# A scratch write between indirect gathers in a two-layer graph kernel

## The chip, the cores and the metric

The kernel runs on one core of a Trainium2 chip. The metric is the device time in microseconds of one execution; lower is better. Besides the times there is a profile of one execution: what each engine ran and when, what ended each wait, and what the DMA queues moved. The engines are named as the profile names them: PE is TensorE (PEld its weight loads), DVE is VectorE, ACT is ScalarE, POOL is GpSimd, SP is SyncE. L191 is line 191 of the kernel before.

## What is computed

A graph of N = 2708 nodes with 128 features each goes through two layers. Each is followed by a residual sum and a normalization over the features. `adj` is a row-normalized adjacency matrix with few entries other than zero in most rows.

Layer 0 is hyperbolic: a product with a 128 x 128 matrix with tanh, artanh and norms around it, then `adj` times the result, then row-wise functions. Layer 1 sends messages along the edges:

```python
s = node_feats @ msg_w[:, :D].T
d = node_feats @ msg_w[:, D:].T
messages = gelu(s[:, None, :] + d[None, :, :] + msg_b)
aggregated = einsum('ijd,ij->id', messages, adj)
new_feats = concatenate([node_feats, aggregated], -1) @ upd_w.T + upd_b
h = gelu(new_feats) + node_feats          # then a layernorm
```

The messages are needed only where `adj[i, j]` is not zero. So the kernel finds the edges, gathers the rows of `d` that belong to them, and works on tiles of 128 edges.

## The kernel before

The nodes lie in NB = 22 blocks of 128. The work has three stages in one program.

*Layer 0, with the search for edges.* For each block b, SP loads a slab `aT` of the transposed adjacency (1.4 MB, L317). TensorE multiplies it with `y` in 22 steps (L324). Beside this ScalarE takes the sign of the slab (L319), and TensorE and VectorE turn the signs into sorted lists of edge positions: `keys` (L350, L358) and `extract`. In `extract` the number of edges per node is summed over the partitions by two small matmuls (L397, L398), ScalarE copies the sums out (L399), VectorE builds 0/1 matrices `R` that assign edge slots to nodes (L409 to L414), and matmuls with `R` (L438) bring each slot its position, from which VectorE works out (L441 to L448) a column index `J` and a flat address `F`. There are 25 lists in all, with 1 to 8 tiles each, 99 tiles together. `F` has three buffers, so a list's addresses can be written only when the gathers of the list three before have taken theirs.

*The end of layer 0* (`layer0_end`) runs in two chunks, blocks 0 to 15 and 16 to 21. It ends with the rows of `d` being written to a table in DRAM by SP (L535), and `s` in `mx` (L534).

*Messages.* For each tile of 128 edges, `dd` receives 128 rows of the table. TensorE spreads `s` over the edge slots (L686), VectorE adds the two (L691), ScalarE applies Gelu (L692), and a matmul with `rv` (built at L688 from the weights `V`) adds the messages up per node (L694). Up to four tiles go together. `dd` comes from a ring of seven buffers, and for the first eight blocks from a slab as well. After each block come the update matmuls (L605 to L608), Gelu (L609), the normalizations and the store (L640). For the first eight blocks the tiles whose columns lie in the first chunk are done ahead, as soon as the table holds these rows.

*The gathers.* GpSimd issues all 198 of them through one helper, `gather`. Ninety-nine fetch one weight of `adj` for each of 128 edges into a column of `V` (L452, 4 bytes for each partition); ninety-nine fetch 128 rows of 512 bytes from the table into `dd` or the slab (L685). They are indirect DMAs: GpSimd makes the descriptors, and the DMA queue moves the data. A gather of `V` waits for its `F`; a gather of `dd` waits for a free buffer; from the ninth on each also waits for the gather eight before it to have landed, since eight semaphores go round.

The order of instructions on each engine is set when the program is built: a scheduler places them by priority and by an estimate of when they become ready, and within an engine they run in that order. `tc.issue_after(ins)` makes the instructions traced inside it stand behind `ins` in the queue of the same engine. It puts them in order; it does not make them wait for the data of a DMA.

Two constants of the setup matter for the change: `ones` (128 x 128 of 1.0, L121) and `nhalf` (one column of -0.5, L124). The last group of the kernel already uses GpSimd for a power, `ve ** -0.5`, at L599, twice, on two columns.

Of the kernel before, what the change touches and what calls it, by code (L numbers as in the profile page):

```python
# [10 lines left out]
F32 = mybir.dt.float32  # L11
# [4 lines left out]
OP = mybir.AluOpType  # L16
AX = mybir.AxisListType

P = 128
# [56 lines left out]
def hyperbolic_then_message_kernel(  # L76
# [10 lines left out]
    nc = tc.nc  # L87
# [11 lines left out]
    const = ctx.enter_context(tc.tile_pool(name="const", bufs=1))  # L99
# [21 lines left out]
    ones = const.tile([P, P], F32, name="ones")  # L121
    nc.gpsimd.memset(ones, 1.0)

    nhalf = const.tile([P, 1], F32, name="nhalf")  # L124
# [62 lines left out]

    of_block = {b: [l for l, v in enumerate(LISTS) if v[0] == b] for b in range(NB)}

    def gather(o, src, at):  # L190
        nc.gpsimd.indirect_dma_start(  # L191
            out=o, out_offset=None, in_=src, in_offset=bass.IndirectOffsetOnAxis(ap=at, axis=0)
        )

    mx = big.tile([P, NB, D], F32, name="mx")
    y = big.tile([P, NB, D + 2], F32, name="y")
# [169 lines left out]
    def extract(l):  # L366
# [84 lines left out]
        for t in range(t0, t0 + n):  # L451
            gather(V[:, t : t + 1], adj.rearrange("i (j o) -> (i j) o", o=1), F[:, t - t0 : t - t0 + 1])  # L452
# [87 lines left out]
    last = {}  # L540
# [135 lines left out]
    def messages(b, ag, tiles, first, final, bins, room=ring):  # L676

        for q, k0 in enumerate(range(0, len(tiles), 4)):
            ts = tiles[k0 : k0 + 4]
            w = len(ts)  # L680
            dd = room(w)
            X = bank(bins[q % len(bins)]).rearrange("p (t d) -> p t d", d=D)[:, :w, :]
            rv = edge.tile([P, 4, P], F32, name="rv", bufs=3)
            for k, t in enumerate(ts):
                gather(dd[:, k, :], table[: SPLIT * P] if t in soon else table, J[:, t : t + 1])  # L685
                nc.tensor.matmul(X[:, k, :], lhsT=R[:, t, :], rhs=s_nm[:, b, :], start=True, stop=True)  # L686

                nc.vector.tensor_scalar(  # L688
                    rv[:, k, :], iotaN, rid[:, t : t + 1], V[:, t : t + 1], op0=OP.is_equal, op1=OP.mult
                )  # L690
            nc.vector.tensor_tensor(dd, X, dd, op=OP.add)  # L691
            nc.scalar.activation(dd, dd, AF.Gelu)  # L692
            for k in range(w):
                nc.tensor.matmul(  # L694
                    ag[:, :P],
                    lhsT=dd[:, k, :],
                    rhs=rv[:, k, :],
                    start=(first and k0 == 0 and k == 0),
                    stop=(final and k0 + k == len(tiles) - 1),
                )  # L700
            step()
# [193 lines left out]
```

## Time and profile before

| | |
|---|---|
| device time, median of 3 runs | 491.01 us (484.5 to 493.97) |
| device time of the profiled execution | 477.53 us |
| span of the profiled execution | 475.8 us |
| granted TensorE clock, mean | 0.83 |
| gathers into V, into dd, into the slab | 99, 81, 18 |
| start of the first and of the last gather | 47.13 and 435.62 us |

The span runs from the first to the last instruction. It splits into a start (to 47 us, where the inputs land and the first list is made), layer 0 with the search (to 253 us, where the first gather from the table starts), the messages (to 437 us, the last gather) and a tail of 39 us. The busy time of each engine in these stretches, in microseconds:

| stretch | PE | DVE | ACT | POOL | granted clock |
|---|---|---|---|---|---|
| 0 to 47 | 26.5 | 33.7 | 24.8 | 11.5 | 0.82 |
| 47 to 132 | 59.2 | 42.3 | 34.2 | 43.4 | 0.86 |
| 132 to 212 | 74.8 | 54.0 | 51.2 | 34.4 | 1.00 |
| 212 to 253 | 37.7 | 34.0 | 28.1 | 8.8 | 0.96 |
| 253 to 437 | 98.4 | 88.0 | 46.5 | 102.9 | 0.73 |
| 437 to 475.8 | 17.0 | 29.7 | 14.2 | 1.4 | 0.76 |

How to read the lines that follow. A group of instructions has its line, engine, operation, what it writes and reads, and a count; after the bar its busy time and the mean of one in ns; after the second bar the idle time of the engine just before these instructions, and what ended most of it. A wait names the instruction that waited, what released it, and the total, the number and the longest. "Remote", or "another core or an unknown queue", means that a semaphore ended the wait and the profile found no instruction that had raised it just then. "Issue" is a wait for which no semaphore was found. On POOL the recorded spans are rough.

### The profile page before, as it was taken

How to read it: one execution, taken by the hardware profiler on the slowest of the kernel's cores; microseconds unless marked ns; L12 is line 12 of the kernel's file. 1: busy time of each engine (PE TensorE's matmuls, PEld its weight loads, DVE VectorE, ACT ScalarE, POOL GpSimd, SP SyncE). 2: the span in 40 equal slices, each digit the busy share in tenths (PEclk: the TensorE clock that was granted, in tenths of full speed). 3: DMA queues.
4: the chain of work that ended last, by engine and by line, in shares of the span. 5: the costliest groups of instructions: out<-in, count | busy, mean ns of one | idle time of the engine just before them, and what ended most of it. 6: DMA issues, size and time to landing. Idle time of an engine off the chain costs nothing.

```text
span 475.8 us, 7804 instructions
## 1 busy us (share of the span) xinstructions
PE 313.6 (66%) x2427; PEld 283.2 (60%) x2427; DVE 281.7 (59%) x1517; ACT 199.0 (42%) x538; POOL 202.4 (43%) x297
## 2 busy tenths in 40 slices
PE   4259778871799999979797402052839755878830
PEld 4259667771789989879686301031839655767720
DVE  1998655552476666689874234714827534566992
ACT  2836344441357565579375111115513311122540
POOL 5300555654454534322225574771351657564001
PEclk9759988977899999999899565575777959789975
DMA  8406322331245544533342011121020112111111
GB/s 331 206 2 214 107 74 95 124 122 44 80 167 201 181 186 160 207 123 123 139 140 72 22 51 31 41 72 28 21 47 12 39 39 53 38 45 34 45 40 39
DMA packets 16236, 45.13 MB, mean 95 GB/s; under 512 B 5626, under 2 KB 11150, under 8 KB 13374
## 3 DMA queue, kind: packets, MB, share of 16 engines
q1 hardware_dynamic: 9710, 37.43, 21.8%
q0 software_dynamic: 6336, 6.55, 5.8%
q10 hardware_dynamic: 144, 0.60, 0.4%
q8 instruction: 20, 0.33, 0.3%
q14 instruction: 26, 0.21, 0.1%
HBM read 41.74 MB, written 2.83 MB: 94 GB/s over the span
## 4 chain that ended last, share of the span: by engine, by line
DVE 29%; PE 25%; another core or an unknown queue 17%; issue 14%; ACT 8%; DMA 4%; POOL 1%; DVEq 0%; POOLq 0%; ACTq 0%
PE mp L324 5%; PE X L686 4%; PE sel L438 3%; PE mp L694 3%; ACT sgn L319 3%; PE kx L350 2%; DVE top L358 2%; DMA V<-in_adj_dram,F 2%; DVE rv L688 2%; PE ag L694 1%; DMA xT<-in_x_t_dram 1%; POOL V L191 1%; PE sel L608 1%; DVE st L592 1%
## 5 line engine op out<-in xcount | busy, mean ns | idle before, releaser
L191 POOL DMA_INDIRECT V<-in_adj_dram,F x99 | 95.1, 961 | 148.9 <-DVE mid L402 34.7
L324 PE MATMUL mp<-y,aT 128*128 128x130 f32 x968 | 127.7, 286 | 1.1 <-DVE y L308 0.9
L324 PEld LDWEIGHTS mp<-y,aT 128*128 128x128 f32 x968 | 118.6, 198 | 1.9 <-DVE y L308 1.1
L191 POOL DMA_INDIRECT dd<-table_dram,J x81 | 76.9, 950 | 76.1 <-issue 20.3
L319 ACT ACTIVATE sgn<-aT 128x2816 bf16<-128x2816 f32 x22 | 56.0, 2548 | 23.1 <-issue 19.0
L438 PE MATMUL sel<-z,R 128*128 128x49 f32 (+4 forms) x198 | 30.8, 295 | 35.8 <-DVE R L412 12.8
L438 PEld LDWEIGHTS sel<-z,R 128*128 128x128 f32 x198 | 27.7, 210 | 38.3 <-DVE R L412 13.0
L686 PE MATMUL X<-mx,R 128*128 128x128 f32 x198 | 35.7, 325 | 17.2 <-DVE mx L534 7.3
L350 PEld LDWEIGHTS <-sgn 128*128 128x128 bf16 x484 | 32.5, 108 | 19.2 <-issue 10.5
L350 PE MATMUL kx<-kd,sgn 128*128 128x128 bf16 x484 | 38.2, 238 | 7.8 <-ACT sgn L319 7.5
L686 PEld LDWEIGHTS X<-mx,R 128*128 128x128 f32 x198 | 31.5, 235 | 19.0 <-DVE mx L534 7.5
L358 DVE MAX8 top<-kx 128x8 f32<-128x128 f32 (+3 forms) x152 | 28.6, 235 | 22.5 <-remote 14.1
L688 DVE TENSOR_SCALAR rv<-iotaN,rid,V 128x128 f32<-128x128 f32 x99 | 30.3, 341 | 14.0 <-remote 6.5
L441 DVE TENSOR_TENSOR work<-sel,place 128x144 f32<-128x144 f32 (+11 forms) x29 | 11.7, 403 | 42.7 <-remote 30.6
L409 ACT ACTIVATE work<-iota,mid 128x512 f32<-128x512 f32 (+3 forms) x53 | 26.8, 553 | 11.2 <-issue 5.7
L444 ACT COPY rid<-sel 128x3 f32<-128x3 f32 (+5 forms) x29 | 4.7, 162 | 55.2 <-DVE work L441 52.3
L691 DVE TENSOR_TENSOR dd<-X,dd 128x384 f32<-128x384 f32 (+3 forms) x29 | 15.1, 524 | 19.5 <-remote 14.8
L694 PE MATMUL mp<-rv,dd 128*128 128x128 f32 x116 | 21.0, 325 | 6.2 <-issue 4.4
L397 PE MATMUL sel<-db,tri 128*128 128x2 bf16 x25 | 4.2, 168 | 27.8 <-ACT db L396 11.8
L694 PEld LDWEIGHTS mp<-rv,dd 128*128 128x128 f32 x116 | 17.9, 229 | 7.6 <-issue 5.1
L692 ACT ACTIVATE dd<-dd 128x384 f32<-128x384 f32 (+3 forms) x29 | 14.0, 499 | 18.8 <-DVE dd L691 15.0
L191 POOL DMA_INDIRECT aT<-table_dram,J x18 | 17.5, 971 | 5.5 <-issue 5.5
(204 smaller groups left out, 580.0 us busy)
## 6 DMA issues: line engine op xcount, KB each, us to landing
aT<-in_adj_t_dram SPq DMA_DIRECT2D x22, 1408.0 KB, 7.2
V<-in_adj_dram,F POOLq DMA_INDIRECT x99
xT<-in_x_t_dram SPq DMA_DIRECT2D x2, 704.0 KB
x_sb<-in_x_nm_dram SPq DMA_DIRECT2D x2, 704.0 KB
out_dram<-nom SPq DMA_DIRECT2D x21, 64.0 KB, 1.6
dd<-table_dram,J POOLq DMA_INDIRECT x81
table_dram<-dt SPq DMA_DIRECT2D x5, 256.0 KB
pk<-in_pack_dram ACTq DMA_DIRECT2D x1, 587.5 KB
```

Of the source, the lines that this page charges most:

```text
L191: nc.gpsimd.indirect_dma_start(out=o, out_offset=None, in_=src, in_offset=bass.IndirectOffsetOnAxis(ap=at, axis=0))
L319: nc.scalar.activation(sgn, aT, AF.Sign, accum_out=signs[:, b : b + 1])
L324: nc.tensor.matmul(op[:, : D + 2], lhsT=aT[:, j, :], rhs=y[:, j, :], start=(j == 0), stop=(j == NB - 1))
L350: nc.tensor.matmul(kp[:, i * P : (i + 1) * P], lhsT=sgn[:, j, :], rhs=kd[:, q, :], start=False, stop=(i == len(groups) - 1 and j == j1 - 1),)
L358: nc.vector.max(top[:, c : c + 8], seg[:, s, :])
L409: nc.scalar.activation(r0, iota[:, k0 * P : k1 * P], AF.Abs, scale=2.0, bias=mid[:, k : k + 1])
L438: nc.tensor.matmul(sp[:, k, :], lhsT=R[:, t0 + k0 + k, :], rhs=z, start=True, stop=True)
L686: nc.tensor.matmul(X[:, k, :], lhsT=R[:, t, :], rhs=s_nm[:, b, :], start=True, stop=True)
L688: nc.vector.tensor_scalar(rv[:, k, :], iotaN, rid[:, t : t + 1], V[:, t : t + 1], op0=OP.is_equal, op1=OP.mult)
L691: nc.vector.tensor_tensor(dd, X, dd, op=OP.add)
L692: nc.scalar.activation(dd, dd, AF.Gelu)
L694: nc.tensor.matmul(ag[:, :P], lhsT=dd[:, k, :], rhs=rv[:, k, :], start=(first and k0 == 0 and k == 0), stop=(final and k0 + k == len(tiles ...
```

## The change

After each gather GpSimd computes one scratch column, `1.0 ** -0.5` for each of the 128 partitions, which nothing reads. The instruction stands directly behind its gather in GpSimd's queue, so that two gathers no longer follow one another at once. All writes go to the same column `gap`, so each also waits for the one before it. The numbers that the kernel computes stay as they are.

```diff
+    gap = const.tile([P, 1], F32, name="gap")
+
     def gather(o, src, at):
-        nc.gpsimd.indirect_dma_start(
+        last = nc.gpsimd.indirect_dma_start(
             out=o, out_offset=None, in_=src, in_offset=bass.IndirectOffsetOnAxis(ap=at, axis=0)
         )
+        with tc.issue_after(last.ins):
+            nc.gpsimd.tensor_tensor(gap, ones[:, :1], nhalf, op=OP.pow)
```

## The prediction

> **What bounds the kernel now.** I read the page first, then the chain of waits, the waits by engine, and the timeline of the places that they name.
>
> ```profile
> PE 313.6 (66%) x2427; PEld 283.2 (60%) x2427; DVE 281.7 (59%) x1517; ACT 199.0 (42%) x538; POOL 202.4 (43%) x297
> DVE 29%; PE 25%; another core or an unknown queue 17%; issue 14%; ACT 8%; DMA 4%; POOL 1%; DVEq 0%; POOLq 0%; ACTq 0%
> L191 POOL DMA_INDIRECT V<-in_adj_dram,F x99 | 95.1, 961 | 148.9 <-DVE mid L402 34.7
> L191 POOL DMA_INDIRECT dd<-table_dram,J x81 | 76.9, 950 | 76.1 <-issue 20.3
> ```
>
> No engine is full, and GpSimd carries 1% of the chain. But 17% of the span, 81 us, hangs on a releaser that the profile cannot name, in a program of one core. The waits by engine say who sits there ("remote" is the same thing):
>
> ```profile
> DVE work L441 <- remote: 30.6, 6, 10.7
> DVE dd L691 <- remote: 14.8, 6, 3.8
> DVE top L358 <- remote: 14.1, 6, 3.9
> ACT dt L532 <- remote: 12.5, 2, 8.1
> ACT nom L609 <- remote: 11.8, 3, 5.7
> ACT oe L399 <- remote: 10.1, 1, 10.1
> ```
>
> The columns are the total, the times and the longest wait. None of these instructions uses what a gather brings in, L691 apart. ACT L399 copies the result of a matmul at L398. The timeline of that place (start, duration, engine, line):
>
> ```profile
> 105.53 0.16 PE L398 MATMUL sel<-db,ones_b 128*128 128x2 bf16 x1
> 106.45 0.95 POOL L191 DMA_INDIRECT V<-in_adj_dram,F  x1 [0.30 <-issue]
> 107.70 0.94 POOL L191 DMA_INDIRECT V<-in_adj_dram,F  x1 [0.30 <-issue]
> 108.94 0.94 POOL L191 DMA_INDIRECT V<-in_adj_dram,F  x1 [0.30 <-issue]
> 110.19 0.94 POOL L191 DMA_INDIRECT V<-in_adj_dram,F  x1 [0.30 <-issue]
> 111.44 0.94 POOL L191 DMA_INDIRECT V<-in_adj_dram,F  x1 [0.30 <-issue]
> 112.69 0.94 POOL L191 DMA_INDIRECT V<-in_adj_dram,F  x1 [0.30 <-issue]
> 116.02 0.16 ACT L399 COPY oe<-sel 128x2 f32<-128x2 f32 x1 [10.13 <-remote]
> ```
>
> The matmul ends at 105.69; its reader starts at 116.02. In between only gathers run, one each 1.25 us. The same picture stands at 52.4 (L438 is done, L441 starts at 55.76, the last gather of that burst at 53.74) and between 279 and 291, where even VectorE's waits for its own results take 1.8 us each. So my reading is: while gathers follow one another, the signals of the other engines arrive late, often only about 2 us after the last gather has started. The profile shows the coincidence, not the mechanism.
>
> The second thing to see is how much slack the gathers have. The timeline of line 691 shows the first quad used at 332.42, its first gather issued at 253.21; the last column is gathered at 435.62 and used at 451.72, 16 us later.
>
> **What the Trainium skill says.** "Perfetto Trace Analysis", section on the SWDGE DMA instruction: the recorded end of such a DMA is the end of descriptor generation, not the landing. The trace agrees: a row lasts 0.94 us, while the chain of waits has a piece of 2.18 us (at 294.36) from issue to landing. The same page, section on GPSIMD engine instructions, says to trust start-to-start spacing rather than spans; I do so below. "SBUF — State Buffer", section on the two sides: a GpSimd instruction that reads SBUF and a VectorE instruction with two SBUF inputs exclude each other for the whole instruction. The new instruction reads two columns, so it can hold up such VectorE work for its own length; before, nothing in the trace tests this. I found no page that says that gathers delay signals.
>
> **The change part by part.** In the order of the built program the other four engines keep their instructions in the same order with the same waits. GpSimd's list goes from gather after gather to gather, power, gather, power: 198 TENSOR_TENSOR on one column are added. Each but the first also waits for GpSimd's own counter, which the power before it raised. Nothing reads the column.
>
> *The price of one pair.* Gather to gather is 1.245 us now (0.944 busy and 0.30 before it). The nearest row to the new instruction is the power at L599 on two columns, 698 and 730 ns, 714 in the mean. A one-column GpSimd instruction (L148) takes 190 ns. If the rest of L599 is per column, one column costs 0.19 + (0.714 - 0.19)/2 = 0.45; if it is fixed, 0.71. I take the middle, 0.58. Two dependent GpSimd instructions at 7.1 and 7.4 us stand 0.08 apart. The pair is 0.94 + 0.08 + 0.58 + 0.30 = 1.90 us. The ends: 1.6, if the 0.30 before a gather passes beside the power, and 2.15, with the dear power and 0.2 in place of 0.08.
>
> *Work added.* 198 x 0.65 = 129 us on GpSimd, about 273 us idle now. Queued behind each power is the next gather, and behind that those who use V and dd. By stage:
>
> - 47 to 253 us: 90 gathers need 90 x 1.90 = 171 of 206 us, so they fit. The waits ended by "remote" here are 19.9 on L441, 10.1 on L399 and 10.2 on L358. The last fall after 132, where TensorE is busy 75 of 80 us and then 38 of 41, so they give back little. Between 47 and 132 TensorE is busy 59.2 of 85: up to 26 us can come back. But 45 gathers at 1.90 need 85 us there, and F has three buffers, so list l waits for the gathers of list l-3. I take 15 of the 26, and 3 us from the end of the first chunk (231 to 246). The first table gather then starts at 253 - 18 = 235.
> - 253 to 437 us: 108 gathers, 135 us at the old pace and 205 at 1.90. Unhindered consumers need less: TensorE is busy 98 of these 184 us, VectorE 88. So GpSimd now sets the pace, and the last gather starts at 235 + 107 x 1.90 = 438, as late as before. What changes is that nobody is behind: 16 us of lag at the end fall away.
> - The tail: landing 2.2, and from the last use to the end 475.8 - 451.7 = 24, of which I take 22 since older groups are done by then. The span is 438 + 2.2 + 22 = 462.
>
> Against 475.8 that is 0.972. On the scale of the median of the runs, 491.0, it gives 477; I say 476.
>
> *The port.* The 198 powers hold 198 x 0.58 = 115 us of GpSimd time; VectorE instructions with two SBUF inputs (L334, L381, L622, L623) are a small part of its 282 us and each loses at most one power. I put it at 0 to 4 us, inside the rounding.
>
> *The wait that is added* is for a power that ended some 1.3 us earlier, so it normally costs nothing. If GpSimd's own signal is late as well, the wait holds the next gather back, which slows GpSimd but gives the others their turn.
>
> **The rivals.**
>
> - *Short pair.* The signals flow and a pair takes 1.65: the first table gather at about 228, the last at 228 + 107 x 1.65 = 405, span 405 + 24 = 429, or 443 on the scale of the runs. For it: the 0.30 may be preparation that does not need the engine. Against it: 0.30 also stands before gathers that follow a long idle time, at 47.13 after F at 46.82.
> - *Long pair: GpSimd becomes the bound and takes it all back.* At 2.1 the first stage gains only about 10 us; the first table gather at 242, the last at 467, span 491, or 507 of the runs, slower by 3%. For it: 0.1 us a pair is worth some 10 to 15 us of span. Against it: it needs both the dear power and a dear hand-over.
> - *The signals stay late.* If it is the share of gathers in time, or if a gap of a micron is too short (in the timeline above the reader starts 3.3 us after the last gather did), the bursts only get longer: half of the 81 us again on top, less the slack of the gathers, 475.8 + 25 = 500, or 516 of the runs. Against it: the gaps of 0.30 are much shorter than the gap of 0.96 between two gathers now, and elsewhere readers start 2.0 us after.
> - *Nothing to gain:* if "remote" were the landing of a gather that is really needed, spacing gathers could only delay. Against it: L399 and L441 wait for TensorE alone in the built program. I count it with the third.
>
> **How the numbers follow.** Forecast 0.45, short pair 0.17, long pair 0.22, signals late 0.16. Faster by over 2%: most of the first (0.36) and all of the second, 0.53. Within 2%: the rest of the first and half of the long pair, 0.20. Slower: 0.27. The range runs from the short pair, 440, to the late signals, 515; a still cheaper pair and a worse jam are left out.
>
> **What would show it.** The spacing of gathers in bursts: 1.90, with a power of about 0.58 in each. The waits "remote": from some 120 us over VectorE and ScalarE down to under 40, no single one over 3. The chain: the unnamed part under 8%, and GpSimd or the landing of dd in its place. The gathers: the first from the table near 235, the last near 438, GpSimd busy near 315 us, and the lag from the last gather to its use down from 16 us to some 3. I am wrong if the long waits stay beside the spaced gathers, or if they go and the span does not follow because a pair takes over 2 us.

## The result and the profile after

The changed kernel takes 460.86 us (median of 4 runs, 460.36 to 465.56) where the kernel before takes 489.13 (4 runs, 484.5 to 493.97). The ratio is 0.947, with an interval of 0.936 to 0.958. The span of the profiled execution falls from 475.8 to 458.6 us. The profiled execution of the kernel before, at 477.53 us, is faster than all four of these runs, so the spans differ by 17 us where the medians differ by 28.

The page of the changed kernel, with its sum line, its chain and the groups on GpSimd and of the messages (lines of the file are 4 higher than before: the gather is L193, the power L197, L441 is L445, L691 is L695):

```profile
PE 327.1 (71%) x2427; PEld 294.5 (64%) x2427; DVE 281.8 (61%) x1517; ACT 198.9 (43%) x538; POOL 331.3 (72%) x495
...
POOL 36%; PE 29%; DVE 15%; issue 8%; DMA 7%; ACT 3%; POOLq 0%; DVEq 0%
POOL gap L197 14%; PE mp L328 9%; POOL V L193 9%; POOL dd L193 9%; POOL aT L193 4%; DMA dd<-table_dram,J 4%; PE mp L698 4%; PE sel L442 3%; PE X L690 2%; DMA V<-in_adj_dram,F 2%; PE kx L354 2%; PE X L532 2%; PE sel L612 2%; DVE top L362 1%; DMA xT<-in_x_t_dram 1%
...
L193 POOL DMA_INDIRECT V<-in_adj_dram,F x99 | 99.4, 1004 | 57.4 <-DVE top L362 31.0
...
L197 POOL TENSOR_TENSOR gap<-ones,nhalf 128x1 f32<-128x1 f32 x198 | 120.7, 610 | 7.1
...
L695 DVE TENSOR_TENSOR dd<-X,dd 128x384 f32<-128x384 f32 (+3 forms) x29 | 15.1, 526 | 63.8 <-DMA dd<-table_dram,J 60.2
```

The unnamed releaser, 17% of the chain before, is gone from it. GpSimd has gone from 1% to 36%, and the power that nobody reads is the longest single line. The wait in front of L695 is now for the landing of `dd`, 60.2 us, where before it was 14.8 us of "remote". The waits by engine (instruction, releaser, total, times, longest; the last line is all that "remote" still ends on VectorE, and none is left on ScalarE):

```profile
DVE dd L695 <- DMA dd<-table_dram,J: 60.2, 17, 17.5
ACT dd L696 <- DVE dd L695: 54.8, 16, 18.4
...
DVE top L362 <- remote: 1.6, 1, 1.6
```

The place where ScalarE stood 10 us for a matmul that was done is L402 and L403 now. The timeline of that list:

```profile
86.18 0.99 POOL L193 DMA_INDIRECT V<-in_adj_dram,F  x1 [0.17 <-issue]
...
87.04 0.16 PE L402 MATMUL sel<-db,ones_b 128*128 128x2 bf16 x1
87.20 0.58 POOL L197 TENSOR_TENSOR gap<-ones,nhalf 128x1 f32<-128x1 f32 x1
87.24 0.16 ACT L403 COPY oe<-sel 128x2 f32<-128x2 f32 x1 [0.42 <-issue]
87.96 1.03 POOL L193 DMA_INDIRECT V<-in_adj_dram,F  x1 [0.18 <-issue]
```

ScalarE follows 0.04 us behind the matmul, and a gather starts every 1.78 us. The third thing to see is a pile:

```profile
306.93 1.12 POOL L193 DMA_INDIRECT aT<-table_dram,J  x1
308.08 15.09 POOL L197 TENSOR_TENSOR gap<-ones,nhalf 128x1 f32<-128x1 f32 x24
323.42 1.00 POOL L193 DMA_INDIRECT dd<-table_dram,J  x1 [0.25 <-issue]
```

Twenty-four powers stand in a row. All powers write one column, so they must run in the order in which the program was traced; the row gathers for the first seven ring buffers are issued before the last weight gathers, but traced after them. So 23 gathers between 230 and 271 us have no power directly behind them, though the change was to put one there, and theirs follow later.

In that stretch gathers still follow one another at 1.25 us, seven from 236.8 and fifteen from 249.7 us on. What is left of late signals in the changed kernel sits there. The one "remote" wait of VectorE ends at 239.67. The others are its waits for its own results:

```profile
264.93 0.94 POOL L193 DMA_INDIRECT dd<-table_dram,J  x1 [0.30 <-issue]
265.55 0.18 DVE L512 BATCH_NORM_AGGREGATE mv<-st 128x2 f32<-128x6 f32 x1 [1.22 <-DVE mv L512]
...
266.17 0.94 POOL L193 DMA_INDIRECT dd<-table_dram,J  x1 [0.30 <-issue]
266.96 0.17 DVE L228 TENSOR_SCALAR c<-c 128x6 int32<-128x6 int32 x1 [1.02 <-DVE c L514]
```

These waits for its own results add up to 12.8 us in the changed kernel, 1.2 at the longest. So "remote" does not count every late signal, and fifteen gathers in a row held nothing back for 10 us here: how late a signal comes is not set by the spacing alone.

Cutting the span of both profiles at the first gather from the table and at the last gather shows where the time went:

| | first row gather | to the last gather | from there to the end | span |
|---|---|---|---|---|
| before | 253.2 | 182.4 | 40.2 | 475.8 |
| changed | 230.1 | 195.9 | 32.6 | 458.6 |

The gain is made in layer 0 (23.1 us) and at the end (7.6 us); the messages got 13.5 us longer.

### The profile page after: what moved, and what is told of

Same layout as the page of the kernel before. It is cut to its first block, busy times and chain, and to the rows that moved or that the text cites. A ratio compares the mean times of both kernels' runs of the same rounds, so it can differ in the third digit from the quotient of the medians.

```text
span 458.6 us, 8002 instructions
## 1 busy us (share of the span) xinstructions
PE 327.1 (71%) x2427; PEld 294.5 (64%) x2427; DVE 281.8 (61%) x1517; ACT 198.9 (43%) x538; POOL 331.3 (72%) x495
## 4 chain that ended last, share of the span: by engine, by line
POOL 36%; PE 29%; DVE 15%; issue 8%; DMA 7%; ACT 3%; POOLq 0%; DVEq 0%
POOL gap L197 14%; PE mp L328 9%; POOL V L193 9%; POOL dd L193 9%; POOL aT L193 4%; DMA dd<-table_dram,J 4%; PE mp L698 4%; PE sel L442 3%; PE X L690 2%; DMA V<-in_adj_dram,F 2%; PE kx L354 2%; PE X L532 2%; PE sel L612 2%; DVE top L362 1%; DMA xT<-in_x_t_dram 1%
## 5 line engine op out<-in xcount | busy, mean ns | idle before, releaser
L193 POOL DMA_INDIRECT V<-in_adj_dram,F x99 | 99.4, 1004 | 57.4 <-DVE top L362 31.0
L197 POOL TENSOR_TENSOR gap<-ones,nhalf 128x1 f32<-128x1 f32 x198 | 120.7, 610 | 7.1
L193 POOL DMA_INDIRECT dd<-table_dram,J x81 | 79.8, 985 | 25.2 <-issue 13.4
L690 PE MATMUL X<-mx,R 128*128 128x128 f32 x198 | 39.3, 343 | 25.1 <-DVE dd L695 23.5
L695 DVE TENSOR_TENSOR dd<-X,dd 128x384 f32<-128x384 f32 (+3 forms) x29 | 15.1, 526 | 63.8 <-DMA dd<-table_dram,J 60.2
L354 PE MATMUL kx<-kd,sgn 128*128 128x128 bf16 x484 | 35.2, 227 | 7.5 <-ACT sgn L323 7.5
L698 PE MATMUL mp<-rv,dd 128*128 128x128 f32 x116 | 29.1, 414 | 16.0 <-ACT dd L696 13.1
L698 PEld LDWEIGHTS mp<-rv,dd 128*128 128x128 f32 x116 | 24.5, 304 | 18.9 <-ACT dd L696 15.1
L692 DVE TENSOR_SCALAR rv<-iotaN,rid,V 128x128 f32<-128x128 f32 x99 | 30.8, 351 | 3.8 <-PE mp L698 2.9
L524 PE MATMUL kx<-ident,x_sb 128*128 128x128 f32 x22 | 5.8, 356 | 21.7 <-DVE x_sb L521 21.4
L452 DVE SCALAR_TENSOR_TENSOR F<-J,rid 128x3 uint32<-128x3 uint32 (+5 forms) x29 | 4.8, 165 | 26.8 <-DMA V<-in_adj_dram,F 18.7
L366 ACT ACTIVATE junk_s<-kx 128x512 bf16<-128x512 f32 (+2 forms) x25 | 14.1, 563 | 15.6 <-DVE top L362 15.4
```

Of the source, the lines that this page charges most:

```text
L193: last = nc.gpsimd.indirect_dma_start(out=o, out_offset=None, in_=src, in_offset=bass.IndirectOffsetOnAxis(ap=at, axis=0))
L197: nc.gpsimd.tensor_tensor(gap, ones[:, :1], nhalf, op=OP.pow)
L354: nc.tensor.matmul(kp[:, i * P : (i + 1) * P], lhsT=sgn[:, j, :], rhs=kd[:, q, :], start=False, stop=(i == len(groups) - 1 and j == j1 - 1),)
L692: nc.vector.tensor_scalar(rv[:, k, :], iotaN, rid[:, t : t + 1], V[:, t : t + 1], op0=OP.is_equal, op1=OP.mult)
L698: nc.tensor.matmul(ag[:, :P], lhsT=dd[:, k, :], rhs=rv[:, k, :], start=(first and k0 == 0 and k == 0), stop=(final and k0 + k == len(tiles ...
```

## The experiments

The kernels of one series ran on one chip, beside fresh runs of the kernel before. One thing has to be told at once, for the numbers can't be read without it: the kernel before took 475 to 499 us in four of the six series (its own first one among them) and 380 to 385 us in the two others, with no run in between. Each time below is therefore set against the kernel before of its own series. The changed kernel ran in two of them only, the first and one further on.

All edits are against the changed kernel, in `gather` and its two calls.

**A short instruction in the gap.**

```diff
-            nc.gpsimd.tensor_tensor(gap, ones[:, :1], nhalf, op=OP.pow)
+            nc.gpsimd.memset(gap, 1.0)
```

> The power in the gap is replaced by a memset of the same column (0.09 us instead of 0.58), in the same places. Theory 'time': the signals of the other engines need some tenths of a microsecond in which GpSimd makes no descriptors; gathers then stand about 1.3 us apart, the unnamed waits come back to over 80 us in VectorE and ScalarE, and the time goes back to 480 to 495 us. Rival 'any instruction between': what helps is that another GpSimd instruction stands between two gathers, however short; the unnamed waits stay under 20 us, gathers stand 1.3 us apart, and the time falls to 425 to 440 us, as GpSimd has 0.5 us less to do for each of 198 gathers.

Measured: 490.71 us (488.35 to 493.4), the kernel before 485.08 (474.69 to 493.17). The ranges overlap: the memset brings nothing. The timeline of this kernel at the same list as above:

```profile
107.21 0.94 POOL L193 DMA_INDIRECT V<-in_adj_dram,F  x1 [0.19 <-issue]
...
107.48 0.16 PE L402 MATMUL sel<-db,ones_b 128*128 128x2 bf16 x1
108.16 0.11 POOL L197 MEMSET gap<- 128x1 f32 x1
108.46 0.94 POOL L193 DMA_INDIRECT V<-in_adj_dram,F  x1 [0.19 <-issue]
...
115.64 0.11 POOL L197 MEMSET gap<- 128x1 f32 x1
118.03 0.16 ACT L403 COPY oe<-sel 128x2 f32<-128x2 f32 x1 [10.14 <-remote]
```

It runs inside the 0.30 us that stood before each gather anyway, so gathers still come every 1.25 us, and the 10 us stall is back at the same copy. "Remote" holds VectorE and ScalarE for 100 us, longest 12.7. So it is not enough that some instruction stands in between.

**A longer instruction in the gap.**

```diff
-    gap = const.tile([P, 1], F32, name="gap")
+    gap = const.tile([P, 6], F32, name="gap")
...
-            nc.gpsimd.tensor_tensor(gap, ones[:, :1], nhalf, op=OP.pow)
+            nc.gpsimd.tensor_tensor(gap, ones[:, :6], nhalf[:, 0:1].to_broadcast([P, 6]), op=OP.pow)
```

> The power works on six columns (about 1.2 us instead of 0.58), so gathers stand about 2.4 us apart. Theory 'GpSimd sets the pace in the changed kernel': 108 row and late weight gathers then take 108 x 0.62 = 67 us longer, and the weight gathers of layer 0 some 20 to 35 us more; 540 to 565 us. Rival 'the signals are still the bound, and a longer gap frees them further': 450 to 475 us, with fewer late signals than in the changed kernel.

Measured: 597.4 us (596.68 to 600.83), in the series of the memset. Above the stated band, on the side of the first theory. The power on six columns takes 1.37 us, so the pair is 2.60: the first row gather comes at 284.8, and the last at 564.8, 280 us later, which is 107 x 2.60 = 278. The waits of this kernel say whose pace it is:

```profile
ACT dd L696 <- DVE dd L695: 123.0, 24, 40.1
DVE dd L695 <- DMA dd<-table_dram,J: 122.3, 19, 39.3
```

**The power only after the weight gathers.**

```diff
-    def gather(o, src, at):
+    def gather(o, src, at, gap_after=True):
...
-        with tc.issue_after(last.ins):
-            nc.gpsimd.tensor_tensor(gap, ones[:, :1], nhalf, op=OP.pow)
+        if gap_after:
+            with tc.issue_after(last.ins):
+                nc.gpsimd.tensor_tensor(gap, ones[:, :1], nhalf, op=OP.pow)
...
-                gather(dd[:, k, :], table[: SPLIT * P] if t in soon else table, J[:, t : t + 1])
+                gather(dd[:, k, :], table[: SPLIT * P] if t in soon else table, J[:, t : t + 1], False)
```

> The power stands only after the 99 gathers of single weights; the 99 gathers of table rows follow one another as in the kernel before. Theory 'the gain is made in layer 0, and in the messages the gap gives and takes alike': the first table gather near 230 us, then the 223 us that the kernel before needs from there; 450 to 460 us. Rival 'late signals in the messages cost more than the pace': the unnamed waits of 25 to 40 us return after 280 us and the time is 468 to 480 us.

Measured: 451.68 us (449.32 to 454.36), same series, in which the kernel before took no less than 474.69. That is faster than the changed kernel in its two series too (460.86 and 461.36), with half of the powers. The first row gather comes at 229.9, as with all powers, and from there to the end it takes 222.2 us, where the kernel before takes 222.6. The late signals are back in the messages, and nowhere else:

```profile
DVE dd L696 <- remote: 20.0, 3, 13.7
ACT dt L537 <- remote: 9.7, 2, 5.3
ACT nom L731 <- remote: 7.8, 1, 7.8
```

Up to the first row gather "remote" holds neither VectorE nor ScalarE at all; after it, 57.5 us. With all powers that stretch takes 228.5 us, and 15 of them are the pile. So in the messages the changed kernel trades one loss for another.

**Without the pile.** As above with the condition `room is ring or quads_in[0] > RING` in place of `False`: the 23 gathers that have no power directly behind them get none.

```diff
-                gather(dd[:, k, :], table[: SPLIT * P] if t in soon else table, J[:, t : t + 1])
+                gather(dd[:, k, :], table[: SPLIT * P] if t in soon else table, J[:, t : t + 1], room is ring or quads_in[0] > RING)
```

> The power is left out after the 23 gathers of rows into the first seven ring buffers, which have none directly behind them in the changed kernel; theirs stand in one pile of 15.1 us at 308. All else as in the changed kernel. Theory 'GpSimd sets the pace from 275 us on': the pile goes and nothing else moves, 445 to 449 us. Rival 'TensorE and VectorE are the bound in that stretch': 456 to 462 us.

Measured: 446.73 us (445.32 to 450.38), same series, the fastest here where signals are late. Twenty-three powers of 0.61 us are 14.0 us; the time is 14.1 below the 460.86 of the changed kernel, which was measured in another series. From the first row gather to the end the profile has 214.6 us, where the kernel with no power in the messages has 222.2: by these two profiles, without the pile the gap pays in the messages too. The chain reads as before the removal, with GpSimd on top:

```profile
POOL 37%; PE 27%; DVE 13%; DMA 9%; issue 9%; ACT 4%; POOLq 0%; DVEq 0%
```

**A second series: shorter gaps, the rows alone, two columns.** The addition and the product replace the power in place. For the rows alone the flag of the edit above goes to the weight gathers' call. For two columns each call names the column that it writes.

```diff
+            nc.gpsimd.tensor_scalar_add(gap, ones[:, :1], 1.0)                       # addition
+            nc.gpsimd.tensor_tensor(gap, ones[:, :80], ones[:, :80], op=OP.mult)     # product, gap [P, 80] bf16
+            nc.gpsimd.tensor_tensor(gap[:, col : col + 1], ones[:, :1], nhalf, op=OP.pow)   # two columns
```

> The power is replaced by an addition of a constant on the same column, an instruction that reads and writes (190 ns for such a one in the kernel before). By the spacings measured so far (1.78 us with 0.58 in the gap, 1.25 us with a memset of 0.1 in it) gathers would stand 1.19 + 0.19 = 1.38 us apart. Theory 'time, and more of it than this': late signals as with the memset, 478 to 492 us. Rival 'it needs an instruction that reads and writes, not time': the signals flow and GpSimd has less to do, 425 to 445 us.

> The power is replaced by a product over 80 columns, written as bf16: an instruction between 0.25 and 0.5 us by the GpSimd rows of the kernel before, so gathers 1.45 to 1.7 us apart. Theory 'the signals flow as soon as a gap of some 0.4 us is there': GpSimd-paced, 1.19 + length per gather, 435 to 455 us. Rival 'it takes the whole 0.6 us': late waits of over 5 us stay in VectorE and ScalarE, 470 to 490 us.

> The power stands only after the 99 gathers of table rows; the 99 weight gathers follow one another as in the kernel before. Theory 'the gain is made in layer 0': the first table gather is back at 248 to 258 us, and from there it takes 220 to 232 us with the power in between; 472 to 490 us. Rival 'the gain is made in the messages': 450 to 465 us.

> The weight gathers' powers write one scratch column and the row gathers' powers another, so that the power of an early row gather no longer has to come behind the powers of weight gathers that stand later in the queue: each gather now has its power directly behind it and the pile of 24 at 308 us goes. The amount of work for GpSimd stays. Theory 'GpSimd sets the pace from 230 us on, whatever the places': the slab gathers start 12 us later, nothing is won, 455 to 463 us. Rival 'the pile itself was the loss': 445 to 450 us.

Measured, with the kernel before at 383.75 us (379.75 to 385.38):

| kernel | time | ratio and interval | gathers apart | first row gather | to the last | to the end |
|---|---|---|---|---|---|---|
| addition | 409.99 | 1.071 (1.060 to 1.083) | 1.44 | 214.9 | 159.8 | 34.0 |
| product | 425.91 | 1.113 (1.102 to 1.125) | 1.50 | 222.1 | 166.7 | 33.7 |
| power, rows only | 436.15 | 1.140 (1.128 to 1.152) | 1.25 and 1.78 | 212.4 | 188.9 | 32.2 |
| power, two columns | 459.19 | 1.199 (1.187 to 1.211) | 1.78 | 235.1 | 193.5 | 32.8 |

Three of the four expectations miss: they took it for granted that unspaced gathers hold back signals. Here they don't. With the power on the rows alone the weight gathers follow one another every 1.25 us, as in the kernel before, and "remote" ends no wait on VectorE or ScalarE. The addition came in below both of its bands: GpSimd has less to do, as its rival had it, but it was not the gap that let signals through; none was held. What this series does show is the price of a gap alone: everything is slower by what GpSimd has more to do. The two-column kernel does the same work on GpSimd as the changed kernel, with no pile, and takes 459, inside the band of its theory. But the changed kernel took its 461 in the other condition, so the two don't show what the places of the powers are worth.

**The changed kernel again.** No edit.

> The changed kernel itself once more, since the second series of variants ran on a chip on which the kernel before took 384 us instead of 485 and no signal came late, although gathers stood 1.25 us apart. Theory 'late signals are a trait of the chip, and the gap only helps where they are late': where the kernel before takes some 384 us, the changed kernel, paced by GpSimd, takes 455 to 464 us as everywhere, 19 to 21 per cent slower; where it takes some 485 us, 455 to 465 us again, 4 to 7 per cent faster. Rival 'something else made that second series fast': the changed kernel falls with the kernel before, to 390 us or less.

Measured: 461.36 us (459.75 to 462.26), the kernel before 492.21 (488.41 to 498.57), ratio 0.939 (0.934 to 0.944), on another chip than the two series before. The result repeats; the condition without late signals did not come up.

**The kernel before, and the addition again.** No edit to either.

> A look at the kernel before on whatever chip this falls on. Theory 'late signals are a trait of the chip': about 384 us, no unnamed wait over 1 us, and gathers 1.25 us apart beside them; or 480 to 495 us with 100 to 130 us of unnamed waits. Nothing in between. Rival 'it varies from run to run on one chip': a time between 400 and 470 us.

> The addition in the gap once more (gathers 1.44 us apart, measured on the chip without late signals, 410 us). If the chip has late signals: theory 'a gap of 0.5 us between the gathers' own spans is enough', 405 to 425 us, 13 to 17 per cent faster than the kernel before; rival 'it takes the 0.84 us that the power makes', 470 to 490 us. If the chip has none: 410 us again, 7 per cent slower than the kernel before.

Measured: the kernel before 385.56 us in the profiled run and 382.61 (379.94 to 385.33) beside it; the addition 410.84 (410.16 to 411.1), ratio 1.073 (1.065 to 1.082). So this series was again without late signals, and its trace shows the unchanged kernel at full flow. The timeline of the list that stalled before, the eighth (L398 and L399 here):

```profile
86.86 0.94 POOL L191 DMA_INDIRECT V<-in_adj_dram,F  x1 [0.31 <-issue]
...
87.21 0.16 PE L398 MATMUL sel<-db,ones_b 128*128 128x2 bf16 x1
...
87.41 0.16 ACT L399 COPY oe<-sel 128x2 f32<-128x2 f32 x1 [0.42 <-issue]
...
88.11 1.05 POOL L191 DMA_INDIRECT V<-in_adj_dram,F  x1 [0.30 <-DMA V<-in_adj_dram,F]
...
89.46 0.94 POOL L191 DMA_INDIRECT V<-in_adj_dram,F  x1 [0.30 <-issue]
```

Same code, gathers 1.25 to 1.35 us apart, and ScalarE starts 0.04 us behind the matmul. No "remote" is left in the waits of this kernel, VectorE waits only 0.6 us for its own results, and the messages already hang on the gathers:

```profile
ACT dd L692 <- DVE dd L691: 24.4, 14, 3.9
...
DVE dd L691 <- DMA dd<-table_dram,J: 16.7, 11, 3.0
```

Its first row gather comes at 213.4, the last 135.6 us later (107 x 1.25 = 134), the end 34.8 us after that.

**The short gap on the weight gathers alone.** As the power only after the weight gathers, with the addition in it.

```diff
+        if gap_after:
+            with tc.issue_after(last.ins):
+                nc.gpsimd.tensor_scalar_add(gap, ones[:, :1], 1.0)
```

> The addition (gathers 1.44 us apart) stands only after the 99 weight gathers; the row gathers follow one another at 1.25 us. On a chip without late signals (kernel before 384 us): layer 0 has room for 1.44 us, its first table gather stays near 214 us, and the messages keep their pace; 383 to 390 us. On a chip with late signals (kernel before 485 to 492 us): theory 'a gap of 0.5 us between the gathers' own spans is enough', first table gather at 225 to 232 us as with the power, 440 to 452 us; rival 'it takes the 0.84 us that the power makes', first table gather past 245 us, 470 to 490 us.

Measured: 460.47 us (455.12 to 469.85), the kernel before 482.39 (475.25 to 493.9), ratio 0.959 (0.925 to 0.993). Late signals again, and on the chip of the two series that had none. So "a trait of the chip" falls; in these six series the condition held through a series and changed between series. And both theories on the length miss: the first row gather comes at 235.0, between their bands. The waits up to there:

```profile
DVE work L446 <- remote: 10.2, 3, 4.8
ACT sgn L324 <- remote: 2.7, 1, 2.7
DVE top L363 <- remote: 2.1, 1, 2.1
DVE nom L333 <- remote: 2.0, 2, 1.9
```

That is 17 us, longest 4.8. Set beside the other kernels in which signals are late, layer 0 gives a graded answer:

| in the gap | weight gathers apart | "remote" on VectorE and ScalarE before the first row gather | first row gather |
|---|---|---|---|
| nothing | 1.25 | 40.2, longest 10.1 | 253.2 |
| memset | 1.25 | 32.5, longest 10.1 | 257.9 |
| addition | 1.44 | 17.0, longest 4.8 | 235.0 |
| power | 1.78 | none | 230.1 |

In this order more time between two gathers goes with fewer late signals, and no sharp threshold shows between 1.25 and 1.78 us. Each row is one profile, and the two at 1.25 differ by 8 us. The kind of instruction changes along with the time: the addition reads and writes a column, and with it 17 us are left, so reading and writing alone is not enough; that the time alone does it is not shown.

## Why the prediction was right, and where it was off

The direction, and the reason given for it, hold for the condition in which both kernels were measured; in the other, of which the forecast knew nothing, the same work on GpSimd only costs time. By its own steps:

- *The reading of "remote".* It was that signals come late while gathers follow at once, and that this costs time. In the series with late signals this holds: the memset kernel keeps an instruction behind each gather but not the time, and the stall of 10 us is back. The kernel before without late signals shows where the reading falls short: there gathers follow at once and nothing is held. So gathers in a row are not enough to make signals late. Predicted: from some 120 us of such waits to under 40, none over 3. Measured: from 120 to 1.6, in one wait, beside the 12.8 us that VectorE waits for its own results (4.0 in the kernel before).
- *The pair.* Predicted 1.90, measured 1.78. The gather's row became 0.99, the hand-over to the power 0.03 instead of 0.08, the power 0.58 as taken, and 0.17 of the 0.30 before the next gather is left. Part of the 0.30 does pass beside the power, as the lower end had it. GpSimd is busy 331 us in all, where near 315 was forecast.
- *Layer 0.* Predicted gain 18, first row gather at 235; measured 23.1, at 230.1. As forecast GpSimd then holds the stage back: gathers of `V` stand on the chain from 84 to 127 us.
- *The order on GpSimd.* This step was wrong. "Gather, power, gather, power" is not what was built: 23 gathers have no power behind them and 24 powers form the pile. It did not spoil the sum, since GpSimd has the same amount to do either way. That 14 us were to be had here the kernel without the pile shows.
- *The messages.* Predicted: GpSimd sets the pace, 203 us from the first row gather to the last. Measured 195.9, which is 107 x 1.78 = 190 and 5 us of delays.
- *The tail.* Predicted 24 us after the last gather, measured 32.6. The lag from the last gather to its use fell from 16.1 to 4.0 as forecast (some 3). But from that use to the end it takes 28.6 us where it took 24.1. TensorE is busy 8.3 us of it, at a granted clock of 0.50, where it was busy 4.0 at 0.62, and the chain stays on it up to 439 us. The forecast had assumed that older groups would be done by then, but VectorE has 117 instructions left in both kernels.
- *The sum.* 230 + 196 + 33 = 459, predicted 462. The errors of layer 0 and of the messages (early by 5 and 7) and of the tail (late by 8) cancel in part, which is luck. The rest of the distance between 476 and 461 is the scaling from a span of 475.8 to the median of 491 of the runs: the kernel before spreads over 484 to 494, but the changed one over 460 to 466 only, and its profiled run, at 460.36, at the low end of that.
- *The port.* Predicted 0 to 4 us. VectorE's busy time went from 281.7 to 281.8.
- *The rivals.* The short pair (1.65, 443 us) was half right: the pair lies between it and the forecast. The long pair and the signals that stay late did not come. But without late signals the same work on GpSimd costs 20%.

What the prediction could not see is that the profile of before shows a condition and not a property of the program. In the other condition its first step is void, and only the cost remains: 21.7 us in layer 0 and 57.9 in the messages (107 x 0.53 = 57) for the two-column kernel, less 2.0 at the end, is the 77.6 between spans of 383.8 and 461.4. The changed kernel itself was not run in that condition. What sets it stays open: nothing in the runs tells the placement of memory, the core, or something else on the chip apart. How gathers hold signals back stays open too; only the dependence on what stands between them is shown. GpSimd's work on a gather, the data that it moves and the number of gathers under way all change with the spacing, and no run takes them apart.

## What to carry to other kernels

If waits end on a releaser that the profile can't name while GpSimd issues gathers back to back, take a second profile in another session before changing the code: here the same program ran at 384 or at 485 us. A gap between gathers buys the signals back at the price of what it adds to their spacing (0.53 us for the power) times the number of gathers, wherever GpSimd sets the pace. Here the weight gathers of layer 0 had the slack for it: the powers behind them alone gave 451.7 us. The fastest kernel where signals are late, at 446.7, kept the powers behind most row gathers too, so try the parts one by one. And a scratch tile that all such fillers share orders them by the program's order; look in the queue for the ones that could not stand where they were meant to.

## What the hardware showed

- The signals of the other engines came up to some 10 us late while gathers were issued every 1.25 us (10.1 us at L399 before and at L403 with the memset). Beside a run of fifteen such gathers in the changed kernel the longest wait on "remote" was 1.7 us (one, in the repeat; none in the first profile), and VectorE waited for its own results at most 1.2 us at a time. In two series of six nothing was late at the same spacing (the kernel before at 385.56 us, and the weight gathers of the kernel with the power on the rows alone).
- A GpSimd memset of 0.11 us between two gathers left their spacing at 1.25; instructions of 0.24, 0.33, 0.58 and 1.36 us made it 1.44, 1.50, 1.78 and 2.60.
- The product over 80 columns, with two inputs in SBUF, came with a longer busy time of VectorE, 293.6 us, against 281.5 with the addition in the same series. The costliest group in both, L692:

```profile
L692 DVE TENSOR_SCALAR rv<-iotaN,rid,V 128x128 f32<-128x128 f32 x99 | 34.2, 393 | 4.1 <-PE mp L698 3.6 <-PE ag L698 0.5
```

```profile
L692 DVE TENSOR_SCALAR rv<-iotaN,rid,V 128x128 f32<-128x128 f32 x99 | 30.7, 358 | 2.4 <-PE mp L698 2.4
```

The first is of the kernel with the product, the second of that with the addition: 35 ns more for each, 3.5 of the 12 us. "SBUF — State Buffer" in the Trainium skill, section "Who interferes with whom", tells of a port pair that GpSimd and VectorE share, and counts VectorE's tensor_scalar among the operations that can take it. That would fit, but the same group took 351 ns with the power, which also reads SBUF and lasts longer, and 356 with nothing in the gap (the kernel before at 385.56 us); no run here took it apart from other causes.
